# Two more of K's seven block products made from quarter products, and VectorE makes the projection's right factors

## The chip, the cores and the metric

The kernel runs on one core of a Trainium2 chip. The metric is the device time of one execution in microseconds, as the median of several runs. TensorE (PE) multiplies; VectorE (DVE), ScalarE (ACT) and GpSimd (POOL) add, copy and apply functions; SyncE (SP) issues the transfers. Each engine has its own row of instructions and waits for the others by semaphores. Products land in PSUM banks. In this kernel there are four tiles of two banks: `s0`, `s1`, `a0` and `a1`, of 128 x 1024 fp32 each.

## The reference

Two attention blocks in sequence, each over 8 images of 512 channels and 1024 positions, all in fp32:

```python
def conv(x, gn, qkv_w, qkv_b, proj_w, proj_b):          # x: (8, 512, 1024)
    xn = group_norm(x) * gn.scale + gn.bias              # 8 groups in layer 0, 32 in layer 1
    q, k, v = split(einsum('oc,bcn->bon', qkv_w, xn) + qkv_b)   # each (8, 512, 1024)
    # 8 heads of 64
    attn = softmax(einsum('bhdi,bhdj->bhij', q, k) / 8, axis=-1)
    out = einsum('bhij,bhdj->bhdi', attn, v)
    return einsum('oc,bcn->bon', proj_w, out) + proj_b + x

x = conv(x, layer 0)
x = conv(x, layer 1)
```

## The kernel before

It works through 16 units (layer, image). A unit has these stages on TensorE, one after the other: the products Q, K and V, the projection of the unit before it, and its own attention. Each 512 x 512 by 512 x 1024 product is made by Strassen's method in Winograd's form: 7 block products in place of 8, with sums around them. They come in the order 1, 6, 2, 7, 5, 4, 3 and use three accumulators, `bx` = `a0`, `by` = `s0`, `bz` = `a1`. A block product made whole is 4 matmuls of 128 x 128 by 128 x 512. In all units but the first, block products 2, 5, 4 and 3 of Q and of K are made by the same method once more: 7 quarter products of 128 x 128 by 128 x 256 in place of 8. The same holds for 2, 3 and 4 of the projection in 13 units.

Quarters 2, 3 and 4 go straight into the accumulator. Quarters 1, 6 and 7 accumulate in turn in one half bank (`one`), and 5 stands in another (`two`). After each of these ScalarE copies the partial sum into a tile `rest`, which GpSimd later adds to the result:

```python
def inner_products(bank, k, one, two, first=False):
    if inner is None or k not in inner:
        products(bank, k, first, not first)              # the whole block product
        return None
    ...
    product(1, one, True, False)
    nc.scalar.copy(rest[:, 0, :FD2], one)
    product(2, bank[:, 0, :FD2], first, True)
    product(3, bank[:, 0, FD2:], False, True)
    product(6, one, False, False)
    nc.scalar.copy(rest[:, 0, FD2:], one)
    product(5, two, True, True)
    nc.scalar.copy(rest[:, 1, FD2:], two)
    product(4, bank[:, 1, :FD2], first, True)
    product(7, one, False, True)
    taken.append(nc.scalar.copy(rest[:, 1, :FD2], one))
    return rest

# [cut] the body of blocks(), the seven block products of one result
products(bx, 1, True, False)
p1 = work(accpool, "acc", "p1")
nc.scalar.copy(p1, bx)
done(sums)
products(by, 6, True, False)
u2 = work(trpool, "tr", "u2")
summed(0, u2, by, p1)                                    # VectorE: u2 = by + bias + p1
done(sums)
rest = inner_products(bx, 2, sbank[1], bz)
c11(bx)                                                  # first quarter of the result, ScalarE for Q and K
add_rest(0, 0, rest)                                     # GpSimd
done(sums)
products(by, 7, False, False)
# [cut] u3
summed(1, u3, by, p1)                                    # VectorE: u3 = by + bias + p1
done(sums)
twice = inner_products(bz, 5, sbank[1], bx, True)
others(1, 1, bz, u3, twice)                              # VectorE: result = bz + u3
# [cut] products 4 into by and 3 into bz, in the same manner
```

`done` counts the block products, 1 to 7 in Q, 8 to 14 in K, 15 to 21 in V, and puts other work between them. Of the unit before, the softmax division of the last heads and its bias stand at 10, which is behind K's block product 2. The sums for the projection stand at 17 to 20:

```python
def divide_last():
    divide(CC - 1)                                       # VectorE: ao = ao * rb, two SBUF inputs
    for h in range(NH):
        add_bias(CC - 1, h)                              # ScalarE, in place on ao

parts = {3: [lambda: reciprocals(CC - 1)], 10: [divide_last], 17: mixing[:2], 18: mixing[2:3], 19: mixing[3:]}
# [cut]
parts[18] += [partial(mix_inner, 2)]                     # GpSimd: 4 differences of 128 x 256 each
parts[19] += [partial(mix_inner, 3)]
parts[20] = [partial(mix_inner, 4)]

# at 2, in every unit: VectorE makes b22 - b12 (needed by Q7) and the right factor of product 4
rest.setdefault(2, []).extend([mixing[3], mixing[2]])
```

The right factors of the quarter products (`r2`, `r5`, `r4`, `r3`, four differences of 128 x 256 each) are made by GpSimd in Q's stage, where they serve Q and K both.

Of the kernel before, what the change touches and what calls it, by code (L numbers as in the profile page):

```python
# [18 lines left out]
P = 128  # L19
# [13 lines left out]
def fast_path(ctx, tc, x, qkv_wT, proj_wT, vecs, groups, out, flag):  # L33
# [27 lines left out]

    INNER, INNER_O = (2, 5, 4, 3), (2, 3, 4)
    assert D == H and C == FD

    def pool(name, bufs, **kw):
# [33 lines left out]
    inner_left, inner_left_o = (  # L99
        [mids.tile([P, n, len(ks), 3, P], F32, tag=f"il{l}{n}", name=f"il{l}{n}") for l in range(2)]  # L100
        for n, ks in ((2, INNER), (1, INNER_O))
    )
# [75 lines left out]
    def mix_inner(u, right):  # L178


        gp = nc.gpsimd
        factors, parts = {}, []
        for k in INNER:
            b = right[k]
            b11, b12 = b[:, 0, :FD2], b[:, 0, FD2:]
            b21, b22 = b[:, 1, :FD2], b[:, 1, FD2:]
            t = ppool.tile([P, 4, FD2], F32, tag="p", name=f"r{k}_{u}")
            t1, t2, t3, t4 = (t[:, i, :] for i in range(4))
            parts += [
                partial(gp.tensor_sub, t1, b12, b11), partial(gp.tensor_sub, t2, b22, t1),  # L190
                partial(gp.tensor_sub, t3, b22, b12), partial(gp.tensor_sub, t4, b21, t2),
            ]
            factors[k] = {1: b11, 2: b21, 3: b22, 4: t4, 5: t1, 6: t2, 7: t3}
        return factors, parts
# [7 lines left out]
    def mix_inner_o(u, right, k):  # L202


        sub = nc.gpsimd.tensor_sub
        b = right[k]
        b11, b12 = b[:, 0, :FD2], b[:, 0, FD2:]
        b21, b22 = b[:, 1, :FD2], b[:, 1, FD2:]
        tag = {2: "x2", 3: "x1", 4: "x4"}[k]
        t = tpool.tile([P, 4, FD2], F32, tag=tag, name=f"ro{k}_{u}")  # L210
        t1, t2, t4 = (t[:, i, :] for i in range(3))
        sub(t1, b12, b11)
        sub(t2, b22, t1)
        sub(b12, b22, b12)
        sub(t4, b21, t2)
        return {1: b11, 2: b21, 3: b22, 4: t4, 5: t1, 6: t2, 7: b12}, t[:, 3, :]

    def mix_inner_left(l, lefts, ks, dst):


        sub = nc.gpsimd.tensor_sub

        def part(n, i, room, after=None):
            left = lefts[i][ks[n]]
            s1, s2, s4 = (room[:, j * P : (j + 1) * P] for j in range(3))
            a11, a12 = left[:, 0, :P], left[:, 1, :P]
            a21, a22 = left[:, 0, P:], left[:, 1, P:]
            first = nc.gpsimd.tensor_add(s1, a21, a22)
            first = getattr(first, "ins", first)
            if after is not None:  # L230
                tc.add_manual_dep(first, name_of(after), DEP, reason="spread over attention")
            sub(s2, s1, a11)
            sub(a21, a11, a21)
            sub(s4, a12, s2)  # L234
            nc.sync.dma_start(dst[l][:, i, n], room.rearrange("p (s o) -> p s o", s=3))

        return [partial(part, n, i) for n in range(len(ks)) for i in range(len(lefts))]
# [6 lines left out]
    def load_inner_left(u):  # L244
# [3 lines left out]
        n = len(INNER) * 3 * P  # L248
        made = []
        for i in range(2):  # L250
            part = flat[:, i * n : (i + 1) * n].rearrange("p (k s o) -> p k s o", s=3, o=P)
            nc.sync.dma_start(part, inner_left[l][:, i])
            made.append({k: [part[:, j, i, :] for i in range(3)] for j, k in enumerate(INNER)})
        return made, flat[:, NT * C - 2 * FD :].rearrange("p (a b) -> p a b", a=2)
# [105 lines left out]
    def blocks(name, left, right, tokens, c11, others, done, u3, summed, inner=None,  # L360
               rests=None, rests_in=None):
# [8 lines left out]
        def products(bank, k, start, stop):  # L370
            a, b = left[k], right[k]
            for i in range(4 if tokens else 2):
# [4 lines left out]
                for c in range(2):  # L377
# [6 lines left out]
                    )  # L384

        def inner_products(bank, k, one, two, first=False):


            if inner is None or k not in inner:
                products(bank, k, first, not first)  # L390
                return None
            left, right = inner[k]
            one, two = one[:, 0, :FD2], two[:, 0, :FD2]
            at, tag = rests_in[k]
            rest = at.tile([P, 2, FD], F32, tag=tag, name=f"m{k}_{name}")

            def product(j, dst, start, stop):
                nc.tensor.matmul(  # L398
                    dst, left[j], right[j], start=start, stop=stop, skip_group_check=True
                )  # L400

            product(1, one, True, False)
            nc.scalar.copy(rest[:, 0, :FD2], one)
            product(2, bank[:, 0, :FD2], first, True)
            product(3, bank[:, 0, FD2:], False, True)
            product(6, one, False, False)
            nc.scalar.copy(rest[:, 0, FD2:], one)
            product(5, two, True, True)
            nc.scalar.copy(rest[:, 1, FD2:], two)
            product(4, bank[:, 1, :FD2], first, True)  # L410
            product(7, one, False, True)
            taken.append(nc.scalar.copy(rest[:, 1, :FD2], one))
            return rest

        def add_rest(r, h, rest, alone=None):

            if rest is not None:
                add = nc.gpsimd.tensor_add
                add(rest[:, 0, FD2:], rest[:, 0, FD2:], rest[:, 1, FD2:])
                add(rest[:, 1, FD2:], rest[:, 1, :FD2], rest[:, 1, FD2:])  # L420
# [6 lines left out]
        products(bx, 1, True, False)  # L427
        p1 = work(accpool, "acc", "p1")
        nc.scalar.copy(p1, bx)  # L429
        done(sums)  # L430
        products(by, 6, True, False)
# [3 lines left out]
        rest = inner_products(bx, 2, sbank[1], bz)  # L435
        c11(bx)
        add_rest(0, 0, rest)
        done(sums)
        products(by, 7, False, False)
        if isinstance(u3, tuple):  # L440
            u3 = work(*u3, "u3")
        else:
            sums.append(u3)
        summed(1, u3, by, p1)
        done(sums)
        twice = inner_products(bz, 5, sbank[1], bx, True)
        others(1, 1, bz, u3, twice)
        add_rest(1, 1, twice, u3)
        done(sums)
        rest = inner_products(by, 4, bx, sbank[1])  # L450
        others(1, 0, by, p1)
        add_rest(1, 0, rest)
        done(sums)
        rest = inner_products(bz, 3, sbank[1], bx)
# [7 lines left out]
    def plain_sum(_, to, bank, more):  # L462
        nc.vector.tensor_add(to, bank, more)  # L463

    def projections(w, rest):
# [13 lines left out]
        for sel, bias in (("q", QB), ("k", KB)):  # L479
            tiles = [  # L480
                qkpool.tile([P, N], F32, tag=sel, name=f"{sel}_{u}_{pr}") for pr in range(CC)
            ]

            def c11(bank):
                for i in range(2):
                    w.last[sel].append(
# [37 lines left out]
            i = "qk".index(sel)  # L524
            left, inner, u3 = w.lefts[i], None, (ppool, "p")
            if w.inner:
                made, u3 = w.made
                inner = {
                    k: (inner_lefts(k, left[k], made[i][k]), w.inner[k]) for k in INNER
                }  # L530
            blocks(
                f"{sel}_{u}", left, w.right, False, c11, others, done, u3, summed, inner,
                rests, {
                    k: (tpool, tag)
                    for k, tag in zip(INNER, (("o1", "o2", "o4", "o1"), ("o4", "o2", "o1", "o4"))[i])
                },
            )
            setattr(w, sel, tiles)
# [6 lines left out]
        def v11(bank):  # L545
# [11 lines left out]
    def project(w, after):  # L557
# [32 lines left out]
        def c11(bank):  # L590
# [14 lines left out]
        def rests(r, h, rest, _):  # L605
# [5 lines left out]

        w.evac = [None, None]
        w.taken = blocks(
            f"o_{w.u}", w.left, w.right_o, False, c11, others, done, (rbpool, "rb"), plain_sum, w.inner_o, rests,
            {2: (tmppool, "tmp"), 4: (tmppool, "tmp"), 3: (accpool, "acc")},
# [28 lines left out]
    def attention(w, at_step, at_end):  # L644
# [201 lines left out]
        src = inner_left_o[l].rearrange("p i k s o -> p (i k s) o")  # L846
# [8 lines left out]
        def mix_inner(k):  # L855
            right, room = mix_inner_o(u, w.right_o, k)
            if k == INNER_O[-1]:
# [4 lines left out]
        def finish():  # L862
            for i, k in enumerate(INNER_O):
# [3 lines left out]
        parts[18] += [partial(mix_inner, 2)]  # L867
        parts[19] += [partial(mix_inner, 3)]
        parts[20] = [partial(mix_inner, 4)]
# [20 lines left out]
    for u in range(2 * B):  # L890
# [4 lines left out]
        rest.setdefault(2, []).extend([mixing[3], mixing[2]])  # L895
        if u > 0:
            w.made = old.made_next
            w.inner, parts = mix_inner(u, right)
            for part in parts[:8]:
                part()  # L900
            rest[2].extend(parts[8:12])
            rest.setdefault(3, []).extend(parts[12:])
# [13 lines left out]
        if u == 0:  # L916
            def first_left_parts():
                for i, part in enumerate(mix_inner_left(0, lefts[:2], INNER, inner_left)):
# [17 lines left out]
        if u == B - 1:  # L936
# [3 lines left out]
            for k in (1, 2, 4):  # L940
                rooms += left_rooms(f"ls{k}", wpool, f"s{k}w2", 2 * FD2)
            made_parts = [
                partial(part, room)
                for part, room in zip(mix_inner_left(1, lefts, INNER, inner_left), rooms)
            ]
        elif u in (1, B + 1):
# [4 lines left out]
                for i, part in zip(  # L951
                    (1, 2, 4), mix_inner_left(units[u][0], [left_o], INNER_O, inner_left_o)
# [7 lines left out]
        if old is not None:  # L960
# [5 lines left out]
            def after(g):  # L966
                stats_of(*stats_after.get(g, ()))
                if u == B - 1:
                    for part in {1: made_parts[:6], 3: made_parts[6:]}.get(g, ()):
# [328 lines left out]
```

## Time and profile before

The median of three runs is 3283.4 us (3280.46 to 3283.47); the profiled execution has a span of 3280.4 us.

| Group of instructions | Count | Mean of one |
|---|---|---|
| TensorE, attention, 64 x 64 by 64 x 512 | 16384 | 589 to 590 ns |
| TensorE, whole block products, 128 x 512 (a part of them) | 256 | 592 ns |
| TensorE, quarter products, 128 x 256 (a part of them) | 240 | 379 ns |
| ScalarE, softmax exponential, 128 x 1024 | 976 | 1023 ns |
| VectorE, softmax row sums, 128 x 1024 | 768 | 1256 ns |
| GpSimd, adding a `rest` to K, 128 x 512 | 120 | 1386 ns |
| ScalarE, copy of a partial sum, 128 x 256 | 45 | 372 ns |
| VectorE, last factor of the softmax division, 128 x 1024 | 64 | 1476 ns |

How to read it: matmuls overlap in the pipeline and their ends are modelled, so a mean is not what one costs; the distance from start to start is. A matmul of fp32 is two records. "a" and "s" are the PSUM tiles, `r` a right factor, `m_q`, `m_k` and `m_o` the tiles called `rest` above, `il` and `lo` left factors, `ao` the output of attention. The number after L is the line in the kernel; a number in brackets at the end of a row is the idle time before it and what ended it. The units repeat every 202 us, with small deviations in three of them.

### The profile page before, as it was taken

What the parts mean: (1) busy time and instruction counts of PE and PEld (TensorE: products, weight loads), DVE (VectorE), ACT (ScalarE), POOL (GpSimd) and SP (SyncE); (2) the same over time, 40 slices, a digit from 0 to 9 for tenths busy, and PEclk for the clock granted to TensorE, in tenths of its full rate; (3) what the DMA queues carried; (4) which work ended last, traced back from release to release, by engine and by line L of the source; (5) the groups of instructions that cost most, each with busy time, mean ns of one, the idle gap of its engine ahead of it and who ended that gap; (6) DMA issues with size and microseconds to landing.
All of it is one profiled execution on the core that took longest, in us unless ns stands there. A gap on an engine that the chain in (4) does not pass through costs nothing.

```text
span 3280.4 us, 55764 instructions
## 1 busy us (share of the span) xinstructions
PE 3250.3 (99%) x21956; PEld 1817.2 (55%) x21956; DVE 2448.9 (75%) x3053; ACT 1627.6 (50%) x2185; POOL 1191.1 (36%) x1260
## 2 busy tenths in 40 slices
PE   7999999999999999999999999999999999999999
PEld 4455474564746547465474645646556464564643
DVE  4876958769586795868958679586795967869577
ACT  1552726537265362744627436274463735637354
POOL 2042171540715317065170602706226072360710
PEclk9999999999999999999999999999999999999999
DMA  2112121121201212013121111201212012120211
GB/s 98 34 40 78 29 85 34 47 78 41 75 31 41 79 41 82 24 66 111 41 85 34 53 61 51 86 15 40 81 45 85 15 41 85 41 85 15 65 73 48
DMA packets 78105, 185.17 MB, mean 56 GB/s; under 512 B 22032, under 2 KB 26768, under 8 KB 77840
## 3 DMA queue, kind: packets, MB, share of 16 engines
q1 hardware_dynamic: 77840, 181.54, 16.3%
q8 instruction: 178, 2.92, 0.4%
q14 instruction: 87, 0.71, 0.1%
HBM read 141.52 MB, written 38.40 MB: 55 GB/s over the span
## 4 chain that ended last, share of the span: by engine, by line
PE 98%; DVE 1%; POOL 0%; DMA 0%; issue 0%; SPq 0%; ACT 0%; POOLq 0%
PE a L705 27%; PE s L677 26%; PE s L380 15%; PE a L380 14%; PE a L398 8%; PE s L398 7%; PE a L677 1%; PE s L625 0%; PE a L625 0%; DMA xn<-x_dram 0%; DVE v L550 0%; POOL x L609 0%; PE a L285 0%; POOL lw L234 0%; DVE s4w L911 0%
## 5 line engine op out<-in xcount | busy, mean ns | idle before, releaser
L685 ACT ACTIVATE p<-s 128x1024 f32<-128x1024 f32 x976 | 997.0, 1023 | 558.6 <-PE s L677 527.7
L705 PE MATMUL a<-p,v 64*64 64x512 f32 x8192 | 1099.6, 589 | 0.1
L677 PE MATMUL s<-q,k 64*64 64x512 f32 x7808 | 1057.8, 590 | 1.4 <-DVE v L550 1.4
L724 DVE TENSOR_TENSOR acc<-acc,p 128x1024 f32<-128x1024 f32 x768 | 964.3, 1256 | 74.1 <-ACT p L685 21.5
L705 PEld LDWEIGHTS a<-p,v 64*64 64x64 f32 x8192 | 383.0, 131 | 496.3 <-ACT p L685 350.9
L677 PEld LDWEIGHTS s<-q,k 64*64 64x64 f32 x7808 | 382.9, 133 | 434.3 <-issue 425.7
L900 POOL TENSOR_TENSOR r<-xn 128x256 f32<-128x256 f32 x30 | 52.2, 1742 | 1135.4 <-DVE acc L724 887.6
L305 POOL TENSOR_TENSOR y<-var,half 128x4 f32<-128x4 f32 x16 | 32.2, 2014 | 439.7 <-DVE var L303 439.7
L722 DVE TENSOR_TENSOR acc<-p,p 128x1024 f32<-128x1024 f32 x128 | 156.6, 1224 | 20.4 <-ACT p L685 16.8
L522 POOL TENSOR_TENSOR k<-k,m_k 128x512 f32<-128x512 f32 x120 | 164.4, 1386 | 0.0
L737 DVE STREAM_TRANSPOSE tr<-acc 128x1024 f32<-128x1024 f32 x128 | 157.9, 1234 | 0.0
L747 DVE TENSOR_REDUCE red<-tr 128x32 f32<-128x1024 f32 x128 | 153.9, 1202 | 0.6
L522 POOL TENSOR_TENSOR q<-q,m_q 128x512 f32<-128x512 f32 x120 | 150.3, 1268 | 0.0
L731 DVE TENSOR_TENSOR ao<-a,tmp 128x512 f32<-128x512 f32 x128 | 87.9, 687 | 65.6 <-ACT tmp L730 65.6
L429 ACT COPY p_o<-a 128x1024 f32<-128x1024 f32 x15 | 15.2, 1012 | 242.9 <-PE a L380 242.9
L463 DVE TENSOR_TENSOR u_v<-s,p_v 128x1024 f32<-128x1024 f32 x32 | 39.2, 1225 | 125.5 <-PE s L380 125.5
L380 PE MATMUL a<-xn,w 128*128 128x512 f32 x272 | 126.2, 607 | 4.4 <-DVE xn L333 4.4
L380 PE MATMUL s<-xn,w 128*128 128x512 f32 x256 | 115.4, 593 | 1.8 <-DVE xn L172 1.8
L380 PE MATMUL a<-w,xn 128*128 128x256 f32 x512 | 115.7, 379 | 0.0
L380 PE MATMUL s<-x_t,s2w 128*128 128x512 f32 x256 | 115.1, 592 | 0.0
L380 PEld LDWEIGHTS a<-w,xn 128*128 128x128 f32 x512 | 97.3, 190 | 13.7 <-issue 0.5
L463 DVE TENSOR_TENSOR u_o<-s,p_o 128x1024 f32<-128x1024 f32 x30 | 36.7, 1225 | 90.4 <-PE s L380 90.4
(282 smaller groups left out, 4686.2 us busy)
## 6 DMA issues: line engine op xcount, KB each, us to landing
rb<-drec SPq DMA_DIRECT2D x128, 256.0 KB, 3.9
il<-il SPq DMA_DIRECT2D x30, 768.0 KB, 5.4
xn<-mid SPq DMA_DIRECT2D x36, 512.0 KB, 7.5
xn<-x_dram SPq DMA_DIRECT2D x32, 512.0 KB, 7.2
x<-x_dram SPq DMA_DIRECT2D x32, 512.0 KB, 4.7
x<-mid SPq DMA_DIRECT2D x28, 512.0 KB, 4.6
mid<-u_o SPq DMA_DIRECT2D x32, 256.0 KB, 2.1
out_dram<-u_o SPq DMA_DIRECT2D x28, 256.0 KB, 2.1
```

The costliest lines, as they stand in the source:

```text
L380: nc.tensor.matmul(dst, at[:, c, ts(i, P)], moving[:, c, :], start=start and c == 0 and not (tokens and i % 2), stop=stop and c == 1, skip ...
L398: nc.tensor.matmul(dst, left[j], right[j], start=start, stop=stop, skip_group_check=True)
L463: nc.vector.tensor_add(to, bank, more)
L522: w.last[sel].append(add(cols, cols, rest[:, i, :]))
L677: nc.tensor.matmul(bank[e * H : (e + 1) * H, j, :], w.k[pr][j * H : (j + 1) * H, t * P + e * H : t * P + (e + 1) * H], w.q[pr][j * H : (j ...
L685: exp = nc.scalar.activation(p, bank, AF.Exp, scale=SCALE)
L705: nc.tensor.matmul(banks[r][j * H : (j + 1) * H, :], w.v[rows, t, lo : lo + D], p[rows, j, :], start=(t == 0), stop=(t == NT - 1),)
L722: nc.vector.tensor_add(acc, state["first"], p)
L724: nc.vector.tensor_add(acc, acc, p)
L731: i1 = nc.vector.tensor_add(w.ao[pr // 2][:, pr % 2, ts(qh, FD)], banks[1], tmp)
L737: nc.vector.transpose(tr, state["acc"].pop(c))
L747: nc.vector.tensor_reduce(red[:, :, qh, :], state["tr"].rearrange("p j (f i) -> p j f i", i=BL), AX.X, ALU.add)
```

## The change

It is meant to take matmuls out of K's stage: block products 1 and 7 of K are made from quarter products too, in 15 units, so K has 6 of 7 made that way. Product 1 serves all four quarters of the result, so its partial sums can't be left to the end: VectorE adds them into `p1` at once. The last quarter of product 1 is issued after the first matmul of product 6, so that its copy has time. As K's result tiles are still empty, they hold the new right factors (`r1` in the fourth, made by GpSimd; `r7` in the third, made by VectorE behind Q's last product) and the partial sums of product 1 (in the second). The orders of the quarters, the half banks and the tiles are now set for each product. To make room on GpSimd, the right factors of the projection's quarter products are made by VectorE in V's stage, in all units but one.

```diff
-    INNER, INNER_O = (2, 5, 4, 3), (2, 3, 4)
+    INNER = {"q": (2, 5, 4, 3), "k": (1, 2, 7, 5, 4, 3), "o": (2, 3, 4)}
...
-        products(bx, 1, True, False)
+        rest = inner_products(bx, 1, True)
         p1 = work(accpool, "acc", "p1")
-        nc.scalar.copy(p1, bx)
-        done(sums)
-        products(by, 6, True, False)
+        if rest is None:
+            nc.scalar.copy(p1, bx)
+            done(sums)
+            products(by, 6, True, False)
+        else:
+            rest, last = rest
+            done(sums)
+            products(by, 6, True, False, last)
+            add = nc.vector.tensor_add
+            add(rest[:, 0, FD2:], rest[:, 0, FD2:], rest[:, 1, FD2:])
+            add(p1[:, 0, :], bx[:, 0, :], rest[:, 0, :])
+            add(p1[:, 1, :FD2], bx[:, 1, :FD2], rest[:, 1, :FD2])
+            add(p1[:, 1, FD2:], rest[:, 1, :FD2], rest[:, 1, FD2:])
         u2 = work(trpool, "tr", "u2")
         summed(0, u2, by, p1)
         done(sums)
-        rest = inner_products(bx, 2, sbank[1], bz)
-        c11(bx)
+        fresh = rest is not None
+        rest = inner_products(bx, 2, fresh)
+        c11(bx, p1 if fresh else None)
         add_rest(0, 0, rest)
         done(sums)
-        products(by, 7, False, False)
+        seventh = inner_products(by, 7)
...
+        if seventh is not None:
+            fold(seventh, seventh[:, 1, FD2:])
...
+        if seventh is not None:
+            rests(1, 1, seventh)
...
+        if seventh is not None:
+            rests(1, 0, seventh)
...
+    ORDER, ORDER_5, ORDER_1 = (1, 2, 3, 6, 5, 4, 7), (1, 5, 2, 6, 3, 4, 7), (2, 3, 1, 4, 5, 6, 7)
...
+            "k": {
+                1: (s1, z, ORDER_1, lambda _: w.k[1].rearrange("p (a b) -> p a b", a=2)),
+                2: (s1, z, ORDER, room_of(tmppool, "tmp")), 7: (z, s1, ORDER, room_of(tpool, "o4")),
+                5: (s1, x, ORDER_5, p), 4: (x, s1, ORDER, p), 3: (s1, x, ORDER, p),
+            },
...
-            def c11(bank):
+            def c11(bank, more):
                 for i in range(2):
+                    if more is not None:
+
+                        n = FD if i == 0 else FD2
+                        w.last[sel].append(
+                            nc.vector.scalar_tensor_tensor(
+                                tiles[i][:, :n], bank[:, i, :n], vec[:, l, bias, i : i + 1],
+                                more[:, i, :n], ALU.add, ALU.add,
+                            )
+                        )
+                        if i == 1:
+                            w.last[sel].append(
+                                nc.scalar.activation(
+                                    tiles[i][:, n:FD], more[:, i, n:], AF.Identity,
+                                    bias=vec[:, l, bias, i : i + 1],
+                                )
+                            )
+                        continue
...
+            engine = nc.gpsimd if u == B - 2 else nc.vector
+            right, room = mix_inner_o(u, w.right_o, k, engine)
...
-            w.inner, parts = mix_inner(u, right)
-            for part in parts[:8]:
+            w.made, w.inner, parts = old.made_next, {}, {}
+            for k in (*INNER["q"], 1, 7):
+                if k in INNER["q"]:
+                    room = ppool.tile([P, 4, FD2], F32, tag="p", name=f"r{k}_{u}")
+                else:
+
+                    room = w.k[{1: 3, 7: 2}[k]].rearrange("p (a b) -> p a b", a=4)
+                engine = nc.vector if k == 7 else nc.gpsimd
+                w.inner[k], parts[k] = mix_inner(right[k], room, engine)
+            for part in parts[2] + parts[5] + parts[1]:
                 part()
-            rest[2].extend(parts[8:12])
-            rest.setdefault(3, []).extend(parts[12:])
+            for g, k in ((2, 4), (3, 3), (7, 7)):
+                rest.setdefault(g, []).extend(parts[k])
...
-                    for part in {1: made_parts[:6], 3: made_parts[6:]}.get(g, ()):
+                    for part in {1: made_parts[:4], 7: made_parts[4:]}.get(g, ()):
```

Shifted: partial left factors for layer 1 are made at other places beside the seventh unit's projection (last lines above), as there are 10 of them now in place of 8. Renamings and the unchanged parts of `inner_products`, which now follows the order it is given, are left out.

## The prediction

> **What bounds the kernel now.** I read the page from the top: busy time by engine, then the chain that ended last.
>
> ```profile
> PE 3250.3 (99%) x21956; PEld 1817.2 (55%) x21956; DVE 2448.9 (75%) x3053; ACT 1627.6 (50%) x2185; POOL 1191.1 (36%) x1260
> ...
> PE 98%; DVE 1%; POOL 0%; DMA 0%; issue 0%; SPq 0%; ACT 0%; POOLq 0%
> ```
>
> TensorE is never without work, so a matmul taken away shortens the kernel and any wait put in front of a matmul lengthens it. The other engines count only where a matmul waits for them. The averages hide how full they are in a stage, so next I read busy time by stretch, for one regular unit (b = 5 of layer 0): its stages Q, K, V and the projection of the unit before.
>
> ```profile
> core 0: us, PE busy (x) PEld busy (x) DVE busy (x) ACT busy (x) POOL busy (x), PEclk, DMA share, GB/s
> 1016.15:1038.66 22.51, 22.51 (x83) 15.13 (x82) 17.39 (x25) 9.68 (x21) 18.69 (x22) 1.00 0.29 96
> 1038.66:1061.04 22.38, 22.38 (x81) 15.12 (x80) 8.05 (x13) 9.35 (x21) 22.07 (x24) 1.00 0.07 23
> 1061.04:1085.22 24.18, 24.18 (x114) 21.28 (x113) 11.18 (x10) 2.40 (x3) 20.80 (x23) 1.00 0.08 25
> ```
>
> K's stage (second row) has GpSimd (POOL) full, 22.07 of 22.38 us, and VectorE (DVE) and ScalarE (ACT) idle for more than half. The change puts work on all three. Last, the order of time in that stage, here TensorE in the middle of it:
>
> ```profile
> 1042.09 3.60 PE L380 MATMUL s<-x_t,s2w 128*128 128x512 f32 x8
> 1045.52 0.59 PE L398 MATMUL s<-xn,w 128*128 128x256 f32 x2
> 1045.95 0.59 PE L398 MATMUL a<-xn,w 128*128 128x256 f32 x2
> ...
> 1048.55 3.60 PE L380 MATMUL s<-xn,w 128*128 128x512 f32 x8
> 1051.98 0.59 PE L398 MATMUL s<-x_t,s1w 128*128 128x256 f32 x2
> ```
>
> Ends on TensorE are modelled, so I use starts. A block product made whole takes 1051.98 - 1048.55 = 3.43 us. One made of 7 quarter products takes 1048.55 - 1045.52 = 3.03 us: 0.432 us a quarter.
>
> What ScalarE and VectorE do in the same stretch matters most for this prediction:
>
> ```profile
> 1047.12 1.86 DVE L787 SCALAR_TENSOR_TENSOR ao<-ao,rb 128x1024 f32<-128x1024 f32 x1
> ...
> 1049.01 1.27 ACT L487 ACTIVATE k<-a,vec 128x512 f32<-128x512 f32 x2
> ...
> 1050.16 1.34 ACT L794 ACTIVATE ao<-ao,vec 128x512 f32<-128x512 f32 x2
> ...
> 1052.73 0.37 ACT L403 COPY m_k<-s 128x256 f32<-128x256 f32 x1 [1.22 <-POOL q L522]
> ```
>
> This is the previous unit's last division (VectorE) and the bias after it (ScalarE). They are put between K's second and seventh products. Before the change they are free: the seventh product is whole and asks nothing of ScalarE, which is next needed at 1052.7.
>
> [...]at 1017.1 two sums of VectorE with both inputs in SBUF took 3.40 us, 1.70 each against 1.22 alone, while GpSimd's 128x256 rows took 1.7 against 0.73; VectorE's rows with one input in PSUM keep 0.415 us (128x256) and 0.69 us (128x512) beside a busy GpSimd. From that I take that alternating rows cost the sum of both less some 0.25 us (1.22 + 0.73 - 0.25 = 1.70).
>
> **The change part by part.** It touches 15 units (all but the first).
>
> 1. K1 and K7 from quarters. Removed from TensorE: 2 x (3.43 - 3.02) = 0.82 us a unit, 15 x 0.82 = 12.4 us. All of it is on the path.
>
> 2. Copies on ScalarE. Each quartered product needs four 0.37 us copies, and quarter 6 may not start until quarter 1 is copied out of the same half bank, because it accumulates on it. Before, such a copy starts 0.69 us after its matmul and ends 0.24 us before quarter 6 (1045.52, 1046.21, 1046.58, 1046.82). That fits when ScalarE is free. For K7 it is not. In the built order of ScalarE the row goes: K2's copies, one quarter of K's first result block (it now needs p1 from VectorE), the two bias rows, and only then K7's copies. The bias rows wait for VectorE's division, and VectorE's order now has the new sums of K1 and the result rows of K2 ahead of it. I time it from the start of K's stage:
> - TensorE: K1's first six quarters 0 to 2.59, K6 with K1's last quarter in it to 6.46, K2 to 9.48. K7's quarter 6 is due at 9.48 + 3 x 0.43 = 10.77.
> - VectorE: Q's last rows end at 0.8. The four new differences for K7's right factors (r7) have two SBUF inputs against a full GpSimd: 4 x (0.415 + 0.73 - 0.25) = 3.6, to 4.4. K1's sums: two rows from PSUM (0.69 + 0.415) and two from SBUF (up to 1.4 each), to about 7.9. The u2 rows, 1.41, to 9.3. K2's result rows, now VectorE's (128x512 and 128x256 from PSUM, together 1.1), to 10.4. The division 1.8 (seen at 1.86 here), to 12.2.
> - ScalarE: bias rows 1.2 from start to next start, so K7's first copy runs 13.45 to 13.8 and quarter 6 starts near 13.9 instead of 10.77: a stall of 3.1 us. If GpSimd blocks VectorE little, r7 and K1's sums end at 5.4, the u2 rows wait for K6 as before (to 8.1), K2's fourth quarter comes at 9.3, the division runs 9.7 to 11.0 and the stall is about 1.8. I take 2.8.
> - Cost: 15 x 2.8 = 42 us.
>
> 3. K1's right factors (r1) on GpSimd: four 0.73 us rows in a gap that was free (3.37 us, 1024.0 to 1027.4). But VectorE makes b22 - b12 for Q7 just there, two SBUF inputs, ending at 1026.0 where Q7 starts at 1026.15. Blocked once it ends some 0.5 us later: 0.35 us on TensorE, 15 x 0.35 = 5 us.
>
> 4. More sums on GpSimd: for K7 a fold (1.45) and four 128x512 additions (5.0), 6.5 us more. With the blocking, K's sums end some 10 us later, near 1082 of this unit. K is read first at 1108, and the reload of x into a buffer they hold is issued at 1082.4: off the path.
>
> 5. The projection's right factors, 12 rows in 12 units, go from GpSimd to VectorE in V's stage: 12 x 0.415 = 5 us into a stage with 24.18 - 11.18 = 13 us free. VectorE's rows that empty banks in V may run late while GpSimd still adds K: V3 accumulates on the bank that V5's result is read from, and I find that margin used up, 0 to 0.6 us. I put 0.25 x 12 = 3 us. Projection stages have no wait to remove but one of 3.2 us (7th unit), of which I give back 1.
>
> Sum: 3283.4 - 12.4 + 42 + 5 + 3 - 1 = 3320 us. I lower it slightly, because the blocking terms are at their upper end: 3317.
>
> **Rivals.**
> - The saving comes through whole: 3283.4 - 12.4 = 3271. For it: TensorE bounds every stage, the copies have their own order of quarters and bank for each product, and work is moved off GpSimd to make room. Against it: the order of ScalarE. It fails only if the division ends two and a half microseconds earlier than I find.
> - VectorE becomes K's limit: r7 and K1's sums so late that K2 or the K6 bank waits too. K2's second quarter writes, at 6.9, a bank half that I have read at 6.4. If blocked rows cost twice what I take, the division ends near 15, the stall is 6 us, and the time about 3283 - 12 + 90 + 8 = 3370. Against it: 1.70 us for a pair is measured.
> - GpSimd's later sums reach the path through the x reload or the projection's first copy. Slack is 8 us or more by the trace; it would add a few us a unit.
>
> **Range and chances.** Stall 1.8 and nothing else gives 3283 - 12 + 27 = 3298; stall 4.4 with 8 us of the small terms gives 3345. Eight in ten: 3295 to 3345. Within 2% is 3218 to 3349. Faster by over 2% would need 65 us where 12 are removed: 1%. Slower by over 2%: 7%. Within: 92%.
>
> **What would show it.** Right: in the chain of waits, TensorE waiting some 2 to 3 us, 15 times, for ScalarE's copy of K7 (tile m7_k), and that copy directly behind the bias rows, which wait for the division; K stages of about 24.4 us where 22.38 minus 0.82 = 21.56 would be unhindered; V's and the projection's stages nearly as before. Wrong: no such wait, then the time is near 3271; or the longest wait sits at K2, K6 or V3 on VectorE, then it is the blocking and not the queue that I misjudged.

## The result, and the profile after

The changed kernel takes 3388.3 us (median of four runs, 3387.4 to 3391.2); the kernel before, on the same chip, 3282.6. The ratio is 1.0324 with a 95% interval of 1.0307 to 1.0342. I predicted 3317 us, 3295 to 3345, and 92% for "within 2%". It is slower by 106 us, where I had expected 34, and outside the range.

The page of the changed kernel, busy time by engine and the chain that ended last:

```profile
PE 3271.7 (97%) x22136; PEld 1864.2 (55%) x22136; DVE 2628.9 (78%) x3347; ACT 1645.8 (49%) x2275; POOL 1273.1 (38%) x1282
...
PE 61%; POOL 19%; issue 12%; DVE 7%; ACT 1%; DMA 0%; POOLq 0%; DVEq 0%; SPq 0%
```

TensorE's share of the last chain fell from 98% to 61%, and GpSimd (POOL), which was on it with 0%, has 19%. GpSimd is busy for 38% of the span, two points more than before: an average that says nothing of what it does to TensorE. TensorE's waits name the places (columns: who waits, for whom, us in total, times, longest):

```profile
PE s L377 <- DVE u_v L479: 42.2, 14, 3.7
PE a L403 <- ACT m_k L408: 39.0, 15, 2.6
...
PE s L403 <- POOL r L518: 3.5, 13, 0.3
PE a L403 <- POOL r L518: 3.0, 13, 0.2
```

The second line is the wait that I had predicted, at K's seventh product (K7), with its count and size. The first (V's seventh product in 13 units, its fourth in one) is as large and in a stage, V, that I had expected "nearly as before". The third and fourth are Q's third product, late by a quarter of a microsecond twice. The same regular unit as in the prediction (b = 5 of layer 0), by stage: Q, K, V.

```profile
core 0: us, PE busy (x) PEld busy (x) DVE busy (x) ACT busy (x) POOL busy (x), PEclk, DMA share, GB/s
1041.46:1065.00 23.54, 23.03 (x84) 15.03 (x81) 18.72 (x25) 9.68 (x21) 23.03 (x25) 1.00 0.30 108
1065.00:1089.43 24.43, 21.83 (x93) 17.39 (x92) 14.77 (x23) 10.55 (x27) 24.04 (x26) 1.00 0.07 22
1089.43:1119.19 29.76, 26.13 (x113) 22.38 (x112) 15.96 (x22) 2.40 (x3) 16.79 (x16) 0.94 0.07 18
```

Before, these stages took 22.51, 22.38 and 24.18 us. K came to 24.43 where I wrote 24.4. Q is 1.03 us longer and V 5.58. The last row has another thing that none of the three had before: a granted TensorE clock (PEclk) of 0.94. Over the span it is 0.994, from 1.00.

Two stretches of the order of time show what the two large waits are. First K7, 10 to 14 us into K's stage:

```profile
1074.24 1.14 DVE L529 SCALAR_TENSOR_TENSOR k<-a,vec,p_k 128x512 f32<-128x512 f32 x2 [1.00 <-PE a L403]
1075.30 1.55 DVE L840 SCALAR_TENSOR_TENSOR ao<-ao,rb 128x1024 f32<-128x1024 f32 x1
...
1076.89 1.33 ACT L847 ACTIVATE ao<-ao,vec 128x512 f32<-128x512 f32 x2 [1.44 <-DVE ao L840]
...
1078.13 0.35 ACT L408 COPY m_k<-a 128x256 f32<-128x256 f32 x1
...
1078.54 0.70 PE L403 MATMUL a<-k,il 128*128 128x256 f32 x2 [2.60 <-ACT m_k L408]
```

It reads downwards: the rows of K's first result block (VectorE, which waited 1.00 us for K2's fourth quarter), division, bias rows, K7's first copy directly behind them, and quarter 6 of K7. ScalarE stood idle for 1.44 us ahead of the bias rows, and the copy, whose quarter had begun at 1074.48, stood behind them (K2's first copy starts 0.64 us after its quarter, K7's 3.65).

Then V's stage, around its own seventh product (V7):

```profile
1101.55 0.72 POOL L575 TENSOR_TENSOR k<-u_k,m_k 128x256 f32<-128x256 f32 x1
1102.31 1.23 DVE L479 TENSOR_TENSOR u_v<-s,p_v 128x1024 f32<-128x1024 f32 x1 [12.08 <-POOL k L575]
...
1103.59 5.41 PE L377 MATMUL s<-w,xn 128*128 128x256 f32 x16 [3.63 <-DVE u_v L479]
1108.83 3.62 PE L377 MATMUL a<-s1w,x_t 128*128 128x256 f32 x16
```

The same three instructions in the kernel before:

```profile
1067.31 0.72 POOL L519 TENSOR_TENSOR k<-u_k,m_k 128x256 f32<-128x256 f32 x1
...
1068.32 1.23 DVE L463 TENSOR_TENSOR u_v<-s,p_v 128x1024 f32<-128x1024 f32 x1 [6.48 <-PE s L380]
...
1071.40 3.62 PE L380 MATMUL s<-w,xn 128*128 128x256 f32 x16
```

V7 overwrites the bank that VectorE empties into V's `u2`, so it waits for that row. The row in turn waits, in the kernel after, for a GpSimd row of K, which V has nothing to do with: 12.08 us of VectorE's idle time end there. What they share is a buffer. `u2` comes from a pool (`tr`) of two buffers in rotation. Q's `u2` has one, K's the other, and K's is read last by that GpSimd row, one of the last sums of K. V's `u2` would take Q's buffer, which has long been free, but at count 15, just ahead of it, the left factors of the projection are loaded into a tile from the same pool and take it. So V's `u2` gets K's. Two units of the changed kernel bear this out: in the second and the tenth these left factors are not loaded, and there V7 does not wait. In the kernel before, GpSimd's row ended at 1068.03, and V7 could have started at about 1069.35 (0.04 us to the `u2` row, 1.28 from there to V7, as in the fence above); TensorE came to it at 1071.40. The slack was 2.05 us. I had looked for the readers of K, and found 8 us.

### The profile page after: what moved, and what is told of

Same layout as the page of the kernel before. It is cut to its first block, busy times and chain, and to the rows that moved or that the text cites. A ratio compares the mean times of both kernels' runs of the same rounds, so it can differ in the third digit from the quotient of the medians.

```text
span 3387.0 us, 56500 instructions
## 1 busy us (share of the span) xinstructions
PE 3271.7 (97%) x22136; PEld 1864.2 (55%) x22136; DVE 2628.9 (78%) x3347; ACT 1645.8 (49%) x2275; POOL 1273.1 (38%) x1282
## 4 chain that ended last, share of the span: by engine, by line
PE 61%; POOL 19%; issue 12%; DVE 7%; ACT 1%; DMA 0%; POOLq 0%; DVEq 0%; SPq 0%
PE a L758 19%; PE s L730 19%; PE s L377 8%; PE a L377 8%; DVE acc L777 4%; POOL k L578 3%; POOL r L967 3%; PE a L403 3%; PE s L403 2%; POOL q L578 2%; POOL r L518 2%; POOL k L967 2%; POOL m_k L417 1%; POOL m_k L416 1%; POOL m_q L417 1%
## 5 line engine op out<-in xcount | busy, mean ns | idle before, releaser
L578 POOL TENSOR_TENSOR k<-k,m_k 128x512 f32<-128x512 f32 x180 | 240.4, 1357 | 0.0
L416 POOL TENSOR_TENSOR m_o<-m_o 128x256 f32<-128x256 f32 x39 | 28.7, 737 | 333.8 <-ACT m_o L408 333.8
L408 ACT COPY m_q<-s 128x256 f32<-128x256 f32 x150 | 55.8, 372 | 159.0 <-PE s L403 149.3
L408 ACT COPY m_k<-s 128x256 f32<-128x256 f32 x165 | 61.4, 372 | 108.4 <-PE s L403 105.1
L377 PE MATMUL s<-w,xn 128*128 128x256 f32 x256 | 71.0, 440 | 41.2 <-DVE u_v L479 41.2
```

Of the source, the lines that this page charges most:

```text
L377: nc.tensor.matmul(dst, at[:, c, ts(i, P)], moving[:, c, :], start=start and c == 0 and not (tokens and i % 2), stop=stop and c == 1, skip ...
L408: taken.append(nc.scalar.copy(to[j], dst[j]))
L578: w.last[sel].append(add(cols, cols, rest[:, i, :]))
```

## The experiments

All of them are the kernel before or after with the edit shown. First theory (A): V7's wait is the reuse of `u2`'s buffer, K7's is ScalarE's queue, Q3's is GpSimd's row, each with its own cause, and taking one away gives back its own microseconds. Rival (C): they stand in one chain, GpSimd's, so that a wait taken away early moves to the next, and only the three together give anything like the saving. Every ratio is to the kernel before, with its 95% interval.

**The load of the left factors one product later.** It then comes behind V's `u2`, which gets Q's buffer.

```diff
-        parts[15] = [load_left]
+        parts[15], parts[16] = [], [load_left]
```

> Only the load of the projection's left factors is placed one block product later (at 16 instead of 15), so that V's u2 takes the buffer of Q's u2 and the load takes the one of K's u2. GpSimd has the same work. Theory A (V7 waits because V's u2 stands in the buffer of K's u2, which GpSimd reads last): the wait of V7 is gone, V's stages are 24.2 us again in place of 25.5 to 29.8, and the time falls by 58 us to about 3330. Rival B (GpSimd's longer queue blocks VectorE's rows in V by contention, whatever the buffers): V's stages stay above 27 us, 3370 to 3390. The wait of K7 stays at 2.6 us, 15 times, under both.

Measured: 3347.8 us, 1.0201 [1.0184, 1.0218].

```profile
PE a L403 <- ACT m_k L408: 39.1, 15, 2.6
...
PE s L377 <- DVE u_v L479: 0.6, 1, 0.6
```

The wait at V7 is gone in all 13 units (the 0.6 us stand at V4 of the tenth), and V's stage is 24.17 us in nine units and up to 25.05 in the rest. This settles the buffer as the cause of V7's wait. It gave back 41 us, where I had expected 58 and the stages of V gave 54: Q and K together grew by 10 us, because the clock now fell behind K7's wait in more units (in nine, where it had been four, Q and K took some 49.6 us or more instead of 48.0), and the projection of the seventh unit waits again (3.0 us).

**The bias rows later, so that ScalarE is free for K7.** The division stays where it is.

```diff
         def divide_last():
             divide(CC - 1)
-            for h in range(NH):
-                add_bias(CC - 1, h)
+
+        def bias_last():
+            for h in range(NH):
+                add_bias(CC - 1, h)
...
-        parts = {3: [...], 10: [divide_last], 17: mixing[:2], ...
+        parts = {3: [...], 10: [divide_last], 14: [bias_last], 17: mixing[:2], ...
...
-    project_last(old, [part for g in (3, 10) for part in rest[g]] + [verdict])
+    project_last(old, [part for g in (3, 10, 14) for part in rest[g]] + [verdict])
```

> Only the two bias rows of ScalarE go from behind K's second block product (10) to behind its last (14); VectorE's division stays at 10. If ScalarE's order is what K7 waits for, the wait of K7 (39 us in all) is gone; if VectorE is too slow as such, a wait of more than 1 us stays. Theory C (GpSimd's sums set when V7 may start, so the waits ahead of it are not added): V7 then waits as much longer, V's stages grow by 2 to 3 us, and the time stays within 8 us of 3388. Rival D (the waits add up): about 3348.

Measured: 3399.8 us, 1.0358 [1.0341, 1.0375]. TensorE's waits of this kernel:

```profile
PE s L377 <- DVE u_v L479: 84.7, 14, 6.4
```

K7's 39.0 us are gone, so the queue of ScalarE was their cause, and the kernel is 11 us slower for it. TensorE comes to V7 2.8 us earlier, GpSimd doesn't, and V7's wait grows from 3.7 to 6.4 us. The waits don't add: each one that is taken away ahead of V7 is paid there, and the longer pauses here cost clock besides (0.987 over the span in place of 0.994). The changed kernel shows it from the other side: in the four units in which the clock fell behind K7, V7 waited 2.0 to 2.2 us in place of 3.6.

**`r1` on GpSimd later**, behind `r3`, so that the rows that Q needs come first.

```diff
-            for part in parts[2] + parts[5] + parts[1]:
+            for part in parts[2] + parts[5]:
                 part()
-            for g, k in ((2, 4), (3, 3), (7, 7)):
+            for g, k in ((2, 4), (3, 3), (3, 1), (7, 7)):
```

> Only K1's right factors go behind those for block product 3 in GpSimd's order. The small waits of Q3 for r3 (6.5 us on the chain, some 13 us with the slow restart) are gone if r1 ahead of it is their cause. Theory C: GpSimd's chain is as long as before, V7 waits longer by the same amount, 3380 to 3390. Rival D: about 3375.

Measured: 3413.5 us, 1.0399 [1.0382, 1.0416]. The two small waits for `r3` are gone, so `r1` ahead of it was their cause; V7's waits are 60.0 us in place of 42.2, the longest 5.6. The gap in GpSimd's row that `r1` had filled stands empty again, and its work for K ends later by the four rows. The direction is that of the chain; the size I missed by 25 us, at the clock (0.987 over the span): it fell behind K7's wait in ten units, where it had been four, and V7 took 5.0 to 6.2 us in all 13 units in which it waited.

**The three moves together.**

> All three moves at once. If the three waits found are all that the change brought, the saving comes through: 3283 less 12.4 us less some 3 us of waits in two units that are gone from the projection, 3268 to 3275. If another wait stands behind them (K2 or V3 on VectorE, the reload of x on GpSimd), the time stays above 3283.

Measured: 3320.0 us, 1.0114 [1.0097, 1.0131]. None of the three waits is left, and the saving is still not there.

```profile
PE a L377 <- DVE v L598: 25.0, 12, 2.1
...
PE a L403 <- ACT m_o L408: 7.9, 1, 7.9
```

V3 now waits for VectorE in 12 units, and the seventh unit's projection waits once. The order of time in V's stage (VectorE, and TensorE at its end):

```profile
1083.21 1.73 DVE L174 TENSOR_TENSOR o_t<-ao,o_t 128x1024 f32<-128x1024 f32 x1 [0.37 <-POOL k L578]
...
1084.87 0.94 DVE L208 TENSOR_TENSOR ro<-ao 128x256 f32<-128x256 f32 x1
...
1085.84 1.38 DVE L209 TENSOR_TENSOR ro<-ao,ro 128x256 f32<-128x256 f32 x1
...
1087.14 0.95 DVE L210 TENSOR_TENSOR ao<-ao 128x256 f32<-128x256 f32 x1
...
1088.01 0.94 DVE L211 TENSOR_TENSOR ro<-ao,ro 128x256 f32<-128x256 f32 x1
1088.88 1.21 DVE L598 TENSOR_TENSOR v<-a,u_v 128x1024 f32<-128x1024 f32 x1
...
1090.14 2.21 PE L377 MATMUL a<-s4w,xn 128*128 128x256 f32 x9 [2.09 <-DVE v L598]
```

Four of the projection's right factors (L208 to L211), which the change gave to VectorE, stand ahead of the row that empties V3's bank. I had them at 0.415 us each; beside GpSimd, still busy with K, they take 0.94 to 1.38. In the changed kernel this lay hidden in the waits ahead of it; with V7's wait alone taken away, V3 waited 1.7 us in five units.

**The projection's right factors later on VectorE** (one product each), and **back on GpSimd**. Both have the three moves, and all left factors of layer 1 at one place.

```diff
 # later on VectorE
-        parts[18] += [partial(mix_o, 2)]
-        parts[19] += [partial(mix_o, 3)]
-        parts[20] = [partial(mix_o, 4)]
+        parts[19] += [partial(mix_o, 2)]
+        parts[20] = [partial(mix_o, 3)]
+        parts[21] = [partial(mix_o, 4)]
 # on GpSimd
-            engine = nc.gpsimd if u == B - 2 else nc.vector
+            engine = nc.gpsimd
 # both
-                    for part in {1: made_parts[:4], 7: made_parts[4:]}.get(g, ()):
+                    for part in {7: made_parts}.get(g, ()):
```

> The three moves, and two more against what stood behind them: VectorE's rows for the projection's right factors go one block product later (19, 20, 21 in place of 18, 19, 20), so that V5's result is read out of its bank ahead of them; GpSimd makes all ten left factors for layer 1 behind the seventh unit's projection (at 7) in place of four of them at 1. Theory E (the order of VectorE in V makes V3 wait 2.1 us in 12 units, and the order of GpSimd makes the seventh unit's projection wait 7.9 us): both waits are gone and the saving of 12.4 us shows at last, 3268 to 3276. Rival F (GpSimd's sums are too long for the unit, the wait only moves once more): 3290 to 3320.

> The three moves and the left factors at 7, but the projection's right factors are made by GpSimd at their old places: the second part of the change is undone. If GpSimd has the time (its K sums end near 1092 in a unit whose projection needs the first of these factors at 1102), V3's wait is gone too and the time is 3268 to 3278, so that VectorE need not have made them. If it has not, block products 2, 3 and 4 of the projection wait for GpSimd, 3290 or more.

Measured: 3280.5 us, 0.9994 [0.9986, 1.0002], and 3279.4 us, 0.9992 [0.9986, 0.9999]. V3's wait is gone in both. That the second is as good shows that this part of the change is not needed: with the waits gone, GpSimd has room for these rows. So the time is that of the kernel before, and neither brought the saving that I had expected. Both still have 8.6 us too many in one place, from the seventh unit's projection to the end of the attention behind it (some 141.7 us where other units take 133.2): there a row for the norm stands on GpSimd behind the ten left factors, and VectorE waits 5.2 us for it.

**The same with one-off places spread out.** As the one before (factors on GpSimd), with the left factors split and one group of weight rows earlier; the lines taken out are those of the changed kernel.

```diff
-                    for part in {1: made_parts[:4], 7: made_parts[4:]}.get(g, ()):
+                    for part in {3: made_parts[:4], 7: made_parts[4:]}.get(g, ()):
...
-            rest.setdefault(16, []).extend(mixing_o)
+            rest.setdefault(12, []).extend(mixing_o)
```

> As the run with the projection's right factors made by GpSimd and the three moves, with two single places mended: four of the left factors for layer 1 go to 3 instead of 7, and VectorE's eight rows of weights in the tenth unit go from V's stage (16) into K's (12). If the 5 us that the eighth unit loses at the start of its attention come from GpSimd's row for the norm standing behind ten left factors, and the 2 us of the tenth unit from those weight rows ahead of V's u3, the time falls from 3279.4 to 3270 to 3275, below the kernel before. If only one of them holds, 3275 to 3278.

Measured: 3275.8 us, 0.9979 [0.9971, 0.9986]. It beats both kernels, by 0.2% of the kernel before. At the seventh unit's projection there are still 4.7 us too many, where the kernel before had 3.5. In a regular unit no wait of TensorE is listed, and yet not all of the 0.82 us arrives. TensorE's starts in the K stage of unit 5 show where it stays: in K1 and in K7 the first quarter that reads the new right factors is followed by the next after 0.54 us in place of 0.43, as a quarter is that had to wait. That is 0.22 us in unit 5, whose K stage took 21.80 us for 22.39; most others took 21.90. All 15 together took 328.4 us for 335.8, and so 7.4 us arrived of 12.4.

**The kernel before, with more work on GpSimd.** This is the buffer alone: behind the sums of one of K's result blocks the kernel before gets four more GpSimd additions of 128 x 512 per unit, into tiles that nobody reads any more, 2 x 2.61 us a unit; the output stays what it was. Nothing is made from quarters that wasn't.

```diff
                         w.last[sel].append(add(cols, cols, rest[:, i, :]))
+                        if sel == "k" and (r, h) == (1, 0):
+                            for _ in range(2):
+                                add(rest[:, i, :], rest[:, i, :], cols)
```

> The kernel before, with nothing of the change but four more additions of 128x512 by GpSimd in each of 15 units, behind K's sums for block product 4, into a tile that nobody reads any more (some 5.0 us a unit; TensorE has exactly the work of before). GpSimd is 36% busy. Theory A: V's u2 waits for GpSimd's last reads of K's u2 with 0.2 us to spare, so V7 waits some 4.8 us in 13 units, and the slower clock after it comes on top: 3345 to 3375. Rival (GpSimd has slack in that stage): 3283 to 3290.

Measured: 3346.4 us, 1.0195 [1.0179, 1.0210]. Its waits:

```profile
PE s L380 <- DVE u_v L463: 44.9, 15, 3.2
```

In unit 5 GpSimd's row ends 12.36 us into V's stage in place of 6.99: 5.37 less the 2.05 of slack is 3.32, and V7 starts 3.30 late. (I had expected 4.8: I had put the slack at 0.2, which is that of `u2`'s row and not of V7.) So 5.2 us a unit on an engine that is busy for 38% cost 64 us: some 47 of delay (15 x 0.17 more than is listed), and most of the rest was lost to a slower clock (0.996 over the span; V7 takes 5.24 us in unit 5).

**The same, with the load of the left factors later** (the first diff above).

> The same four additions, and the projection's left factors loaded one block product later, so that V's u2 no longer takes the buffer that GpSimd reads last. Theory A: V7's wait is gone. A smaller wait may stand behind it, as the projection's second difference takes a tile that GpSimd reads last and VectorE stands still for it: 3283 to 3310. Rival B: as without the move, 3345 or more.

Measured: 3324.7 us, 1.0128 [1.0112, 1.0143]. V7's wait is gone, and there is one behind it, longer than the small one that I had allowed for:

```profile
1087.09 1.73 DVE L172 TENSOR_TENSOR o_t<-ao,o_t 128x1024 f32<-128x1024 f32 x1 [5.66 <-POOL k L522]
1088.75 1.21 DVE L463 TENSOR_TENSOR u_v<-s,p_v 128x1024 f32<-128x1024 f32 x1
...
1090.01 3.22 PE L380 MATMUL s<-w,x_t 128*128 128x256 f32 x7 [1.96 <-DVE u_v L463]
```

A sum for the projection (`o_t`) goes into a buffer that held partial sums of K, which GpSimd reads last. VectorE waits there for 5.66 us, and V's `u3` behind it, with V4 behind that: 29.1 us in 15 units. By the trace and the order of allocation it is the same mechanism a second time, in another pool; no run moved this one.

**K1 alone and K7 alone from quarters.**

```diff
 # K1 alone
-    INNER = {"q": (2, 5, 4, 3), "k": (1, 2, 7, 5, 4, 3), "o": (2, 3, 4)}
+    INNER = {"q": (2, 5, 4, 3), "k": (1, 2, 5, 4, 3), "o": (2, 3, 4)}
 # K7 alone
+    INNER = {"q": (2, 5, 4, 3), "k": (2, 7, 5, 4, 3), "o": (2, 3, 4)}
```

(The right factors of the product that is left out are not made either.)

> The changed kernel with K1 from quarters and K7 whole again. TensorE saves 6.2 us. GpSimd loses 6.4 us of sums a unit, so Theory A expects that V's u2 waits 1 to 2 us where it waited 3.6; K7's wait is gone, as nothing asks ScalarE behind the bias rows; Q3's waits stay. 3295 to 3330. If K1's sums on VectorE were the main cost: 3360 or more.

> The changed kernel with K7 from quarters and K1 whole again. TensorE saves 6.2 us, r1 is gone from GpSimd and K1's sums from VectorE. Theory A: K7 waits still, 2.0 to 2.6 us behind the bias rows; V7 waits 3 to 5 us for GpSimd, and Q3's waits are gone: 3365 to 3395. If K1 were the main cost: below 3330.

Measured: K1 alone 3288.1 us, 1.0016 [1.0009, 1.0023]; K7 alone 3370.3 us, 1.0266 [1.0250, 1.0282]. K7 is what costs: it alone has both waits.

```profile
PE s L377 <- DVE u_v L479: 41.5, 14, 3.2
PE a L403 <- ACT m_k L408: 27.2, 15, 1.8
```

In K7 alone K7's wait is 1.8 us in place of 2.6, and the division has no part in it: it ends at 1070.6, before ScalarE comes to the bias rows. ScalarE makes two rows of K's result there (1.27 us, from 1071.25), the bias rows follow at once (1072.40), and the copy behind them (1073.63). The queue alone costs 1.8. With K1 from quarters too, VectorE makes three quarters of these result rows ahead of the division, which so begins later, and ScalarE waits for it (the 1.44 us above). I had expected 1 to 2 us at V7 with K1 alone and there was none: K1's partial sums go to VectorE, and GpSimd's row ends 8.17 us into V's stage in place of 6.99, later by less than the slack of 2.05. The 6.2 us that K1 alone removes are spent at Q's third product: 7.3 us of listed waits, and Q's stages took 355.3 us in 15 units for 340.1.

**K1 alone, with `r1` later.**

> K1 alone from quarters, K7 whole, and r1 behind r3 in GpSimd's order. If r1's place was all that K1 cost (Q3's waits, 1.1 us a unit), the saving of 6.2 us is left, with some 3 us of one wait in the eighth unit that was gone without K7 too: 3272 to 3277, below the kernel before. If GpSimd's lateness only moves to V7, as with both products, 3285 or more.

Measured: 3295.3 us, 1.0034 [1.0022, 1.0046]. The small waits in Q are gone and Q and K take 672.9 us in 15 units, 3.0 less than before the change; but V7 waits again:

```profile
PE s L377 <- DVE u_v L479: 15.8, 14, 1.1
```

GpSimd stands idle for 3.37 us in Q's stage as in the kernel before, and its row for `u2` ends 10.35 us into V's stage in place of 6.99: 3.36 later, less the slack of 2.05, is 1.31, and V7 starts 1.29 late. So in these two orders one of the two is paid: `r1` in that gap, late for Q3, or behind it, late for V7. Of my two forecasts the second came true, not the saving.

## Why the prediction was wrong

The difference of the spans is 3387.0 - 3280.4 = 106.6 us. Delays are start to start, and so some 0.2 us longer than the listed wait (2.87 for 2.60 at K7). I had lowered my sum of 37 to 34. Of the some 70 us that I missed, 45 are the wait at V7 (step 4), 18 the clock and 9 the delay of Q (step 3).

| Term | Predicted | Measured |
|---|---|---|
| Matmuls saved | -12.4 | -12.4 removed |
| K7 behind the bias rows | 42 | 15 x 2.87 = 43 |
| Q delayed by `r1` | 5 | 13 x 1.05 = 14 |
| V7 waits for `u2`'s buffer | 0 | 42.2 + 14 x 0.17 = 45 |
| Slower clock after the pauses | 0 | 7 x 1.7 + 4 x 1.6 = 18 |
| V3 (projection's factors) | 3 | 0 |
| Seventh unit's projection | -1 | -3 |
| Sum | 37 | 105 |

- **Step 1** (saving): right in what it removes. The spread version shows that 5.0 of the 12.4 us were lost again in K's stages, nearly all without a listed wait.
- **Step 2** (ScalarE's queue): the queue is right (K7's first copy stood behind the bias rows, and with these moved K7's 39.0 us were gone), and the size nearly so: I had the division end 12.2 us into the stage and quarter 6 at 13.9; they are at 11.85 and 13.54. What made the division late is not what I wrote, and there is luck in the number. `r7` ended at 4.6 us for 4.4, but K1's sums at 6.9 for 7.9 and the `u2` rows at 8.2 for 9.3, and then VectorE waited 1.00 us for K2's fourth quarter, in all 15 units. So TensorE, and not GpSimd's blocking of VectorE, set when the result rows and the division could begin (9.24 and 10.30 us into the stage). The rows did slow each other: `r7`'s took 0.83 to 1.26 us beside GpSimd, where I had 0.9 each and rows of that shape take 0.42 in this unit's V stage with GpSimd idle (from 1111.31), and four of GpSimd's 128x256 rows beside them took 0.78 to 0.91 for 0.72.
- **Step 3** (`r1`): right engine, wrong victim. I thought that VectorE's b22 - b12 would be blocked by it. That row took its 1.22 us, and Q7 was on time; GpSimd was the one held up: two of `r1`'s four rows took 1.82 and 1.71 us for 0.73, so that they did not fit into the gap of 3.37. Its next right factor, `r3`, came 1.5 us later, and two quarters of Q3 waited. 1.05 us a unit for 0.35.
- **Step 4** failed: "K is read first at 1108, and the reload of x into a buffer they hold is issued at 1082.4: off the path". Counted from Q's start, GpSimd's chain came 8.9 us later (1.5 from `r1`, 1.0 where its rows were held up beside VectorE's new ones, 6.4 from K7's sums). That is even less than the 10 I allowed. Q and K grew by 3.1 us, so relative to V's start it came 5.85 later. But the slack was not 8 us: it was 2.05, since the first to need what GpSimd holds is not a reader of K; it is V's `u2`, through a buffer of a rotating pool. 5.85 - 2.05 = 3.80, the delay seen at V7 in this unit. The third rival named GpSimd and two ways to the path, and both were the wrong ones.
- **Step 5** (V3's bank): the mechanism is right and was hidden. With all three waits gone it costs 2.1 us in 12 units where I put 0.25: I took VectorE's rows at their undisturbed 0.415 us in a stage where GpSimd is still busy, after having used the disturbed figure, 0.9, in step 2.
- **The clock** was in no step. The time lost by a pause of TensorE was taken as the pause.

## What to carry to other kernels

Where one engine is busy for 99%, ask of every other engine how late its last read of each rotating buffer may come, and who takes that buffer next by the order of allocation: here a load allocated one product earlier tied V's second sum to K's last. Waits in one chain don't add; taking away an early one moved it to the last, at a loss, and only taking away the last one, or all of them, paid. Give a pause of TensorE more than its length, since the clock may fall behind it (where it did here, that cost 1.5 to 1.7 us more in the changed kernel and 2.0 to 2.5 with the bias rows later).

## What the runs showed of the hardware

A pause of TensorE of 2 to 3 us was at times enough to slow it. In the changed kernel's unit b = 2 of layer 0, behind K7's wait:

```profile
449.39 1.20 PE L403 MATMUL a<-k,il 128*128 128x256 f32 x2 [2.61 <-ACT m_k L408]
450.38 1.06 PE L403 MATMUL s<-k,il 128*128 128x256 f32 x2
451.24 1.06 PE L403 MATMUL s<-k,w 128*128 128x256 f32 x2
```

The quarters come 0.99 and 0.86 us apart in place of 0.54 and 0.43, as they do in unit 5 after the same wait: half speed, and the granted clock (PEclk) from 449.46 to 452.86 is 0.50. In the changed kernel it was so for 3.4 us at a time and lost 1.5 to 1.7 us each time: in four of 15 units at the end of K7's wait, and in seven of the nine in which V7 waited 3.6 us (in unit 5 V7 took 1108.83 - 1103.59 = 5.24 us for 3.45, and the granted clock from 1104.82 to 1108.22 is 0.50). Over the runs it came more often behind longer pauses: none of 13 of 1.1 us (K1 alone with `r1` later), none of 15 of 1.8 us (K7 alone, at K7), 5 of 12 of 2.1 us (the three moves, at V3), and all 13 of 6.4 us (bias rows later), which lost 2.0 to 2.5 us each. Length does not decide alone: 2.6 us at K7 slowed it in nine of 15 units with the load later, and some 3.1 us at V7 in all 13 with K7 alone, but in seven of 13 in the kernel before with more work on GpSimd. What decides which pauses are hit these runs do not show.

A quarter product that has had to wait takes 0.53 to 0.54 us to the next start in place of 0.43 (1078.54 to 1079.07 behind K7's wait in unit 5), and its listed wait is some 0.17 us short of the delay. Many short waits so cost more than their sum.
